# Adding the last stage's result to a tensor that already lies in the output: an accumulating DMA in place of load, add and store

## The chip, the cores and the metric

The kernel runs on one core of a Trainium2 chip. The metric is device time in microseconds, from the first to the last instruction with what lies around them; the figure for a kernel is the median over several runs. All engines of the core take part: TensorE (PE) for products, VectorE (DVE), ScalarE (ACT) and GpSimd (POOL) for elementwise work, SyncE (SP) for issuing transfers, and 16 DMA engines that carry every transfer, whichever queue issued it.

## The reference

Input x has shape (8, 256, 56, 56) in float32. Two layers are computed, each as a residual on top of a group norm `_gn`:

```
x1  = x  + involution(gn(x))             # 7x7 involution, 16 groups
out = x1 + block(gn(x1))                 # two convolutions with ternary weights

def block(v):
    out1 = relu(batch_norm(conv_tri(v, w1), g1, b1))
    out2 = batch_norm(conv_tri(out1, w2), g2, b2)
    return relu(out1 + out2)
```

`batch_norm` uses the statistics of the whole batch, so no element of `out1` is known before the first convolution has been done for all eight images, and no element of `out` before the second has. With y1 and y2 for the raw results of the two convolutions, and sc1, bi1, sc2, bi2 for the scale and bias that follow from the statistics (one pair for each channel), the last step is

```
out = x1 + relu(sc2*y2 + bi2 + relu(sc1*y1 + bi1))
```

## The kernel before

The work is done in four stages, one after the other. Stage 1 computes the involution image by image and quarter by quarter of the channels, with GpSimd, VectorE and ScalarE around the products, and stores its result x1 (`store_x1`, L888) into tensors in DRAM. Stages 2 and 3 are the two convolutions (`conv_phase`, L356), each over 16 half images. They load x1 or y1 from DRAM (`load`, L345), transform it (a Winograd form along the rows), multiply on TensorE, and store y1 or y2 to DRAM (L565). The results have to lie in DRAM because the batch's statistics come at the end of a stage[...].

The last stage, from L1079, is the one that the change touches. It runs over 16 tiles, one for each image b and half t of the channels. A tile has 128 partitions (channels) and 3136 columns (the 56 x 56 points), 1568 KB. The last two tiles are cut along the columns, into two and four pieces, so that the tail is short. For each piece it

- loads y1, y2 and x1 by three DMAs from SP's queue (L1098),
- applies scale, bias and ReLU to y1 on ScalarE (L1099),
- forms sc2*y2 + y1 on VectorE, in place in y1 (L1100),
- applies the bias and ReLU on ScalarE (L1101),
- adds it to x1 on VectorE (L1102), in place in x1,
- stores x1 to the output by a DMA from ScalarE's queue (L1103).

y1 and y2 have two buffers each and x1 three. They lie in four pools, fa to fd, placed one behind the other from the bottom of the memory that stage 3 leaves; `homes` (L1083) says which tile of which tensor lies in which pool: fd takes the first of each tensor, fa, fb and fc the others. Where a pool lies decides what it waits for at the start: the memory under it holds stage 3's loaded rows (rawp), its weights (wqa with the first four groups, wqb with the last two), the padded image (pad) and temporaries (tmpp). In the kernel before, fd lies over pad and tmpp, which are free before the last products are; fb lies over wqa.

The order of instructions on each engine is set by the Tile scheduler in this stage, engine by engine, with semaphores for data and buffers. SP's queue works in order: a load that waits for its buffer holds up those behind it.

Of the kernel before, what the change touches and what calls it, by code (L numbers as in the profile page):

```python
# [11 lines left out]
ALU = mybir.AluOpType  # L12
# [5 lines left out]
P = 128  # L18
B, C, H, W = 8, 256, 56, 56
HW = H * W  # L20
CT = C // P
# [68 lines left out]
def involution_tri_block_kernel(  # L90
# [3 lines left out]
    nc = tc.nc  # L94
    out = out.rearrange("b c h w -> b c (h w)")
# [5 lines left out]
    def scratch(name):  # L101
        return [[dram.tile([P, HW], F32, tag=f"{name}_{b}_{t}", name=f"{name}_{b}_{t}")
                 for t in range(CT)] for b in range(B)]

    x1_d, y1_d, y2_d = scratch("x1d"), scratch("y1d"), scratch("y2d")
    wq_d = [dram.tile([P, QS * CT * 3 * C], F32, tag=f"wqd{i}", name=f"wqd{i}") for i in range(2)]


# [970 lines left out]
    with ExitStack() as ph4:  # L1079

        fa, fb, fc, fd = (ph4.enter_context(tc.tile_pool(name=name, bufs=1))
                          for name in ("fa", "fb", "fc", "fd"))
        homes = {"y1": (fd, fa), "y2": (fd, fb), "x1": (fd, fb, fc)}  # L1083

        def home(name, j):
            k = j % len(homes[name])
            return homes[name][k].tile([P, HW], F32, tag=f"{name}{k}", name=f"{name}f_{j}")


        for j in range(B * CT):  # L1090
            b, t = j // CT, j % CT
            y1f, y2f, x1f = (home(name, j) for name in ("y1", "y2", "x1"))
            n = {B * CT - 2: 2, B * CT - 1: 4}.get(j, 1)
            f = HW // n
            for cols in (slice(k * f, (k + 1) * f) for k in range(n)):
                y1, y2, x1 = y1f[:, cols], y2f[:, cols], x1f[:, cols]
                for v, src in ((y1, y1_d), (y2, y2_d), (x1, x1_d)):
                    nc.sync.dma_start(v, src[b][t][:, cols])  # L1098
                nc.scalar.activation(y1, y1, AF.Relu, bias=bi1[:, t:t + 1], scale=sc1[:, t:t + 1])  # L1099
                nc.vector.scalar_tensor_tensor(y1, y2, sc2[:, t:t + 1], y1, ALU.mult, ALU.add)  # L1100
                nc.scalar.activation(y1, y1, AF.Relu, bias=bi2[:, t:t + 1])  # L1101
                nc.vector.tensor_tensor(x1, x1, y1, ALU.add)  # L1102
                nc.scalar.dma_start(out[b, t * P:(t + 1) * P, cols], x1)  # L1103


# [84 lines left out]
```

## Time and profile before

| | |
|---|---|
| median of 3 runs | 2163.53 us (2159.11 to 2166.13) |
| the profiled execution: time | 2164.76 us |
| the profiled execution: span, first to last instruction | 2163.0 us |
| DVE busy in the whole span | 1753.4 us (81%) |
| DMA traffic | 440.06 MB in 156250 packets, mean 203 GB/s |
| HBM read, written | 323.28 MB, 112.20 MB |
| last product (L522) ends, last stage's first y1f step on DVE (L1100) | 1927.3 us, 1933.03 us |
| L1099, L1100, L1101, L1102 from 1936 us on: busy | 43.5, 56.6, 47.7, 55.3 us |
| the same on a whole tile | 3.00, 3.48, 2.91, 3.43 us |
| loads of a whole tile y1f, y2f, x1f: issue to landing, median | 14.4, 18.6, 25.2 us |
| store of a whole tile out_y: issue to landing, median | 11.8 us |

The profile is one execution as the hardware profiler recorded it. "Busy" is the time in which an engine executed instructions, without the instructions that only issue transfers. A row such as `L1100 DVE ... y1f<-y2f,sc_bn,y1f` names the line of the kernel, the engine, and what is written from what. "Issue to landing" runs from the instruction that issues a transfer to the moment at which its semaphore says that all of it has arrived, with the time that it stands behind other transfers. The DMA share is the mean busy share of the 16 DMA engines in a stretch of time; GB/s counts each byte moved once.

### The profile page before, as it was taken

The numbers are of one execution on the slowest core, as the hardware profiler recorded it, in microseconds if no ns is written. First come the engines' busy times: TensorE is split into PE (matmuls) and PEld (weight loads), VectorE is DVE, ScalarE is ACT, GpSimd is POOL, SyncE is SP. The second block draws the span as 40 slices with busy tenths as digits, with TensorE's granted clock in tenths as the row PEclk, the third lists the DMA queues.
The fourth block names the chain that finished last, engine by engine and source line by source line (L and its number), as shares of the span: only waits on it lengthen the run. The fifth ranks groups of instructions, "written<-read, shape, count | busy, mean of one in ns | idle before, by whom it ended". The sixth has DMA issues, their size and how long they took to land.

```text
span 2163.0 us, 70724 instructions
## 1 busy us (share of the span) xinstructions
PE 1759.3 (81%) x29680; PEld 1632.6 (75%) x29680; DVE 1753.4 (81%) x3337; ACT 1432.2 (66%) x3553; POOL 590.7 (27%) x965
## 2 busy tenths in 40 slices
PE   4988988989899898988699999997999999960000
PEld 4777777878777687777699999997999999960000
DVE  5777978787777868877699999998999999984444
ACT  3877787877767677777366666665566666653344
POOL 0555566555546646666200000000000000000000
PEclk9999999999989999999799999998999999985555
DMA  5667777686767758667733333335323333369999
GB/s 184 212 178 232 220 211 236 195 266 197 244 185 218 239 164 263 191 203 201 254 122 122 122 122 122 122 122 189 118 114 124 124 128 128 124 262 425 429 428 397
DMA packets 156250, 440.06 MB, mean 203 GB/s; under 512 B 63774, under 2 KB 74012, under 8 KB 148508
## 3 DMA queue, kind: packets, MB, share of 16 engines
q1 hardware_dynamic: 150336, 405.50, 55.2%
q10 hardware_dynamic: 5596, 30.03, 3.3%
q8 instruction: 235, 3.85, 0.8%
q14 instruction: 83, 0.68, 0.1%
HBM read 323.28 MB, written 112.20 MB: 201 GB/s over the span
## 4 chain that ended last, share of the span: by engine, by line
PE 68%; DMA 10%; DVE 9%; issue 6%; POOL 3%; ACT 3%; ACTq 0%; SPq 0%; POOLq 0%; DVEq 0%
PE c L522 40%; PE pg L820 14%; PE pa L852 8%; PE pk L713 3%; DMA y1f<-y1d 3%; DMA x1f<-x1d 2%; PE ks L786 2%; DMA out_y<-x1f 2%; POOL q L751 1%; DVE x1f L1102 1%; DVE inv L864 1%; ACT a L824 1%; DMA y2f<-y2d 1%; POOL x L868 1%; DMA q<-in_x_nb 1%
## 5 line engine op out<-in xcount | busy, mean ns | idle before, releaser
L522 PE MATMUL c<-pl,wq 128*128 128x392 f32 x4608 | 857.7, 348 | 14.9 <-ACT pl L392 14.9
L522 PEld LDWEIGHTS c<-pl,wq 128*128 128x128 f32 x4608 | 855.7, 190 | 16.7 <-ACT pl L392 15.3
L824 ACT ACTIVATE a<-pg,bt 126x126 f32<-126x126 f32 (+1 forms) x2048 | 530.1, 469 | 110.1 <-PE pg L820 109.5
L820 PE MATMUL pg<-kr,wl 64*126 64x140 f32 (+1 forms) x6144 | 466.1, 296 | 41.2 <-issue 16.4
L820 PEld LDWEIGHTS pg<-kr,wl 64*126 64x126 f32 x6144 | 405.5, 198 | 67.2 <-issue 24.3
L852 PE MATMUL pa<-a,q 126*32 126x48 f32 x17024 | 290.4, 215 | 67.0 <-issue 52.6
L852 PEld LDWEIGHTS pa<-a,q 126*32 126x32 f32 x17024 | 242.1, 116 | 135.4 <-issue 83.6
L828 DVE TENSOR_TENSOR a<-pg,bt 126x504 f32<-126x504 f32 (+4 forms) x640 | 280.9, 480 | 54.4 <-PE pg L820 52.8
L868 POOL TENSOR_TENSOR x<-x,inv 128x168 f32<-128x168 f32 x320 | 167.0, 522 | 404.1 <-DVE inv L864 370.7
L864 DVE SCALAR_TENSOR_TENSOR inv<-pa,gn1s,inv 128x168 f32<-128x168 f32 (+1 forms) x384 | 134.2, 351 | 154.6 <-ACT inv L862 151.1
L392 ACT CAST pl<-r 128x812 fp32r<-128x812 f32 x192 | 162.5, 868 | 143.4 <-DVE r L387 122.8
L372 POOL MEMSET xp<- 128x116 f32 x32 | 6.3, 196 | 826.1 <-DVE a L387 826.1
L751 POOL TENSOR_TENSOR q<-q,sides 126x256 f32<-126x256 f32 (+1 forms) x320 | 225.5, 705 | 3.1 <-DMA q<-in_x_nb 3.1
L393 DVE TENSOR_TENSOR pl<-r,pl 128x812 fp32r<-128x812 f32 x192 | 186.6, 998 | 27.6 <-ACT pl L392 26.3
L457 ACT ACTIVATE dummy<-y,nc 128x1568 f32<-128x1568 f32 (+1 forms) x128 | 200.2, 1564 | 4.8 <-DVE y L542 3.5
L862 ACT ACTIVATE inv<-pa,gn1s 128x168 f32<-128x168 f32 x320 | 134.9, 423 | 69.5 <-PE pa L852 49.3
L149 DVE BATCH_NORM_STATS2 st<-x 128x6 f32<-128x392 f32 x256 | 137.8, 554 | 16.4 <-DMA x<-in_x 10.1
L800 POOL TENSOR_TENSOR x<-x,add 128x504 f32<-128x504 f32 (+1 forms) x128 | 127.2, 1024 | 25.4 <-ACT add L794 25.4
L1049 ACT ACTIVATE xp<-raw,gn 128x392 f32<-128x392 f32 (+1 forms) x124 | 82.5, 721 | 61.3 <-DVE a L387 61.0
L1069 ACT ACTIVATE xp<-raw,bi_bn,sc_bn 128x392 f32<-128x392 f32 (+1 forms) x124 | 82.3, 720 | 58.8 <-DVE a L387 57.1
L1100 DVE SCALAR_TENSOR_TENSOR y1f<-y2f,sc_bn,y1f 128x3136 f32<-128x3136 f32 (+2 forms) x20 | 56.6, 2831 | 64.6 <-DMA y2f<-y2d 50.6
L713 PE MATMUL pk<-x,wrn 64*128 64x168 f32 (+1 forms) x1152 | 101.0, 316 | 0.0
(174 smaller groups left out, 1789.2 us busy)
## 6 DMA issues: line engine op xcount, KB each, us to landing
q<-in_x_nb SPq DMA_DIRECT2D x320, 448.0 KB, 4.2
raw<-x1d SPq DMA_DIRECT2D x32, 812.0 KB, 5.9
raw<-y1d SPq DMA_DIRECT2D x32, 812.0 KB, 6.1
x<-in_x SPq DMA_DIRECT2D x64, 392.0 KB, 5.3
x1d<-x SPq DMA_DIRECT2D x64, 392.0 KB, 5.2
y1d<-y SPq DMA_DIRECT2D x30, 784.0 KB, 3.7
y2d<-y SPq DMA_DIRECT2D x30, 784.0 KB, 3.4
y1f<-y1d SPq DMA_DIRECT2D x14, 1568.0 KB, 14.4
```

The source lines that it names most:

```text
L392: nc.scalar.copy(hi, r)
L393: nc.vector.tensor_tensor(lo, r, hi.bitcast(F32), ALU.subtract)
L457: nc.scalar.activation(dst, v, f, bias=shift[:, to:to + 1], accum_out=stats[:, to, j, n:n + 1])
L522: nc.tensor.matmul(ps[:, to, :NM], wq[k][:, t, dx, to * P:(to + 1) * P], part[:, t, :, dx:dx + W], start=(c == 0), stop=(c == last))
L713: nc.tensor.matmul(ps[h][:, :m * W], wrn[rows, c, :], src[rows, r0:r0 + (m - 1) * PY + 1:PY, :], start=(c == 0), stop=(c == NCQ - 1))
L751: nc.gpsimd.tensor_tensor(v, v, z, ALU.add)
L820: nc.tensor.matmul(dst, wl[rows, c, gp, o:o + NQ], kr[py][rows, px, :], start=True, stop=True)
L824: nc.scalar.activation(dst[:, g + 1, p0 + j], ps[1][:NQ, j * nt + t0:j * nt + t1], AF.Identity, bias=bt[:, c, g + 1, p0 + j:p0 + j + 1])
L828: nc.vector.tensor_tensor(dst[:, g, p0:p0 + n].rearrange("q p t -> q t p"), ps[0][:NQ, t0 * n:t1 * n].rearrange("q (t p) -> q t p", p=n), ...
L852: nc.tensor.matmul(ps[o:o + m, k * w:(k + 1) * w], q[:NQ, k, o:o + m], av[:, t + k, g * w:(g + 1) * w], start=True, stop=True)
L864: nc.vector.scalar_tensor_tensor(iv, parts[:, :, g], scale[:, g:g + 1], iv, ALU.mult, ALU.add)
L868: nc.gpsimd.tensor_tensor(xv, xv, iv.rearrange("p t (y x) -> p y t x", x=PX), ALU.add)
```

## The change

x1 no longer has tensors of its own in DRAM. It is stored into the output tensor, and stages 2's loads of x1 read it from there. In the last stage x1 is not loaded and not added on VectorE: y1, which holds the rest of the sum after L1101, is sent to the output by a DMA with `accum_op=ALU.add`, issued from GpSimd's queue, which adds it to what lies there. The argument `max_dma_last_dim` limits a piece of a transfer to 1568 floats, so a row of 3136 goes as two pieces. The third buffer in fc, which was x1's, is given to y1: y1 has three buffers, y2 two, and fd holds two tiles instead of three, so fc and fd lie lower in memory than before: fc over wqa, fd over wqb and pad.

```diff
-    x1_d, y1_d, y2_d = scratch("x1d"), scratch("y1d"), scratch("y2d")
+    y1_d, y2_d = scratch("y1d"), scratch("y2d")
+    x1_d = [[out[b, t * P:(t + 1) * P, :] for t in range(CT)] for b in range(B)]
...
-        homes = {"y1": (fd, fa), "y2": (fd, fb), "x1": (fd, fb, fc)}
+        homes = {"y1": (fd, fa, fc), "y2": (fd, fb)}
...
-            y1f, y2f, x1f = (home(name, j) for name in ("y1", "y2", "x1"))
+            y1f, y2f = (home(name, j) for name in ("y1", "y2"))
...
-                y1, y2, x1 = y1f[:, cols], y2f[:, cols], x1f[:, cols]
-                for v, src in ((y1, y1_d), (y2, y2_d), (x1, x1_d)):
+                y1, y2 = y1f[:, cols], y2f[:, cols]
+                for v, src in ((y1, y1_d), (y2, y2_d)):
                     nc.sync.dma_start(v, src[b][t][:, cols])
                 nc.scalar.activation(y1, y1, AF.Relu, bias=bi1[:, t:t + 1], scale=sc1[:, t:t + 1])
                 nc.vector.scalar_tensor_tensor(y1, y2, sc2[:, t:t + 1], y1, ALU.mult, ALU.add)
                 nc.scalar.activation(y1, y1, AF.Relu, bias=bi2[:, t:t + 1])
-                nc.vector.tensor_tensor(x1, x1, y1, ALU.add)
-                nc.scalar.dma_start(out[b, t * P:(t + 1) * P, cols], x1)
+                nc.gpsimd.dma_start(out[b, t * P:(t + 1) * P, cols], y1, accum_op=ALU.add,
+                                    max_dma_last_dim=4 * min(f, HW // 2))
```

The order of the instructions on the engines, as the scheduler sets it, is the same before the last stage. In the last stage, tile 1 comes before tile 0 on VectorE and in the accumulations; SP issues y1 of tile 1, the last two y2 stores, y2 of tile 1, y1 of tile 2, then y1 and y2 of tile 0; GpSimd has nothing between its last memset of the convolution and the first accumulation. One line is added near the top, so the lines after it have numbers that are higher by one.

## The prediction, made before the changed kernel had run

> **What bounds the kernel now.** Only the last stage changes its work, so I read first the page's slices, to see when that stage runs and what is full in it:
>
> ```profile
> PE   4988988989899898988699999997999999960000
> DVE  5777978787777868877699999998999999984444
> ACT  3877787877767677777366666665566666653344
> POOL 0555566555546646666200000000000000000000
> DMA  5667777686767758667733333335323333369999
> GB/s 184 212 178 232 220 211 236 195 266 197 244 185 218 239 164 263 191 203 201 254 122 122 122 122 122 122 122 189 118 114 124 124 128 128 124 262 425 429 428 397
> ```
>
> A slice is 54 us. In the last four TensorE is silent, DVE and ACT are under half busy, GpSimd does nothing, and the DMA row stands at 9: the stage is bound by transfers. Second, the windows, for the rate in the stage's steady part, and beside it five microseconds of the convolution in which the engines are as full:
>
> ```profile
> core 0: us, PE busy (x) PEld busy (x) DVE busy (x) ACT busy (x) POOL busy (x), PEclk, DMA share, GB/s
> 1861.00:1866.00 5.00, 5.00 (x29) 5.00 (x28) 5.00 (x6) 5.00 (x7) 0.00 (x0) 1.00 1.01 360
> 1953.00:2143.00 190.00, 0.00 (x0) 0.00 (x0) 88.42 (x27) 77.01 (x28) 0.00 (x0) 0.50 1.01 427
> ```
>
> The last stage moves rows of 12,544 bytes at 427 GB/s with a DMA share of 1.01. The window at 1861 holds loads whose rows are 6,496 bytes (812 KB over 128 partitions): the same full engines move only 360 GB/s. So a full engine pays 427/360 = 1.19 times as much for a byte in half-length rows. Third, the waits from 1936 us on:
>
> ```profile
> ACT y1f L1099 <- DMA y1f<-y1d: 69.8, 16, 10.6
> ACT y1f L1101 <- DVE y1f L1100: 61.2, 18, 5.0
> DVE y1f L1100 <- DMA y2f<-y2d: 50.6, 13, 5.5
> DVE x1f L1102 <- DMA out_y<-x1f: 27.6, 7, 4.0
> ```
>
> Columns: who waited for whom, total us, times, longest. The heads of both compute engines' loops wait for loads; the rest is the chain inside a tile. Last, the timeline of SP's queue shows when the stage's loads begin:
>
> ```profile
> 1910.71 0.80 SPq L565 DMA_DIRECT2D y2d<-y  x2
> 1912.33 0.32 SPq L1098 DMA_DIRECT2D y1f<-y1d  x1
> 1912.70 1.25 SPq L1098 DMA_DIRECT2D y2f<-y2d  x1
> 1914.00 0.92 SPq L1098 DMA_DIRECT2D x1f<-x1d  x1
> 1918.43 0.32 SPq L1098 DMA_DIRECT2D y2f<-y2d  x1
> 1918.79 0.43 SPq L1098 DMA_DIRECT2D x1f<-x1d  x1
> ```
>
> **The unit.** A tile is 128 x 3136 floats, 1.606 MB; at 427 GB/s it takes 3.76 us. A tile of output costs four such units now (y1, y2, x1 in, out), 15.04 us. The timeline agrees: L1099 starts at 2010.09 and, seven tiles later, at 2115.35, which is 15.04 us each. The whole stage agrees too: from 1912.33 there are 47 loads, 16 stores and one tile of last y2 stores left, 64 units or 240.6 us, which ends at 2152.9; the span ends at 2163.0, so some 10 us are gaps at the start and the tail at the end.
>
> **What the Trainium skill says.** "DMA: Bandwidth & Descriptors", section "Issuing engines are not separate DMA queues": transfers issued from SP, ACT and GpSimd run on the same 16 engines and interleave. So moving the store to GpSimd's queue gives no bandwidth. The trace of before has no transfer from GpSimd to test it. "Collectives: The Full Stack", section "The bandwidth ceiling: the fold count and why AG ≠ RS ≠ AR": an adding transfer reads two sources for each write, both on the same read ring, and a reducing transfer measured 62.28/32.35 = 1.93 times as long as a copy. No run here shows it yet; it is the central unknown. "DMA: Bandwidth & Descriptors", "Anatomy of one DMA — SWDGE (gpsimd) path" puts about 2 us of fixed time on such a transfer; here the last out_y, 392 KB or 0.94 us of data, is issued at 2159.63 and the span ends 3.4 us later, so fixed time is about 2.4 us on ACT's queue too.
>
> **The change part by part.**
> Removed: 20 loads of x1 (16 tiles, 16 units), 20 plain stores (16 units), 20 DVE additions, 55.3 us busy. The additions are worth nothing but the last one's 0.98 us, because DVE waits for loads; in their absence DVE would wait longer for y2. The store issues on ACT (0.36 us each) likewise.
>
> Added: the accumulating transfer, 16 tiles in 20 instructions. It reads y1 from SBUF, reads out in HBM and writes out. Call its price a units a tile. From below: if the destination's read cost the engine nothing, a = 1. Two reads at the full rate: a = 2, or 1.93 by the skill. But the changed line also cuts a row into two pieces of 1568 floats, 6,272 bytes, near the rows of the 1861 window; with that window's 1.19, a = 2 x 1.19 = 2.37. From above: if read, add and write of a piece don't overlap, the source's and the destination's reads and the write stand behind each other and the add's own turn adds something, a = 3 to 4. I take 2.37, the only value that uses both a reason for two reads and this trace's own rate for pieces of this length. HBM traffic gives no relief: three tiles read and one written, before and after.
>
> Moved: stores go past nothing on GpSimd, whose last memset is at 1881.91. An accumulation waits there for the final ReLU (L1101), and behind it stand only later accumulations. Who waits for it: SP, because a y1 buffer now comes free only when the accumulation has landed, where before the DVE addition freed it. SP is in order, so a y2 load can stand behind such a wait. Is three y1 buffers enough? One turn is load about 10 us, ACT, DVE and ACT 3.0 + 3.5 + 2.9 = 9.4, some 6 of waiting between them, and an accumulation that shares the engines, about 2 x 2.37 x 3.76 = 18: 43 us. Three buffers at the transfers' pace, (2 + 2.37) x 3.76 = 16.4 us a tile, allow 49. So transfers stay the bound.
>
> Moved too: the pools. The pool fd holds two tiles, not three, and slides down onto wqb, the weights of the last two matmul groups; y1 and y2 of tile 0 can be loaded only after the last matmul, 1927.35, not at 1912.33. Instead y2 of tile 1 and y1 of tile 2 go at 1918.4. The x1 that now lies in out has the same rows of 12,544 bytes and the same stores and loads earlier in the kernel: I cost that at nothing, since those transfers have the same shapes and the convolution runs with a DMA share near 0.35.
>
> **The sum.** From 1918.4 the queues hold 31 loads (all but y1 of tile 1) and one tile of y2 stores: 32 units, 120.3 us. Accumulations: 16 x a x 3.76 = 60.2 a; at 2.37, 142.6. Gaps: 1.0 start of the first load, 1.5 until the last matmul frees wqb (two loads end at about 1926.9, the next begin at 1928.4), about 2 before the first accumulation, about 1.5 when y2 stands behind y1 on SP, and 2 of landing at the end: 8. Span: 1918.4 + 120.3 + 142.6 + 8 = 2189.3. The profiled execution took 2164.76 for a span of 2163.0, so 1.8 lie outside; its time is 1.2 above the median 2163.53. So 2189.3 + 1.8 - 1.2 = 2189.9, say 2190: 1.2% slower. In general 2047.3 + 60.2 a. Break-even is a = 1.93.
>
> **Rivals.**
> Faster: the destination's read is hidden, because source and destination are read from different memories at once, so an accumulation costs one write's worth. a = 1 to 1.19 gives 2107.5 to 2118.9; at a = 1 three buffers pace the stage at about 12 us a tile instead of 11.3, which adds some 4: 2111. It decides from a below 1.82. For it: four units became three transfers. Against it: the 1.93 of the skill. Chance 0.20.
> No change: two reads, but no loss by the shorter pieces, a = 1.9 to 2.0: 2161.7 to 2167.7. The transfers that go are paid back by the second read. For it: the skill's ratio is exactly the break-even. Against it: 360 against 427 GB/s. Chance 0.12.
> Much slower: the addition stands in the way, as read, read and write that don't overlap. a = 3 gives 2227.9, a = 4 gives 2288. For it: nothing in this trace; against it: the skill's 1.93. Chance 0.20.
> GpSimd becomes the bound: it must write descriptors for 256 pieces a tile; beyond 16.4 us a tile, 64 ns a piece, it would set the pace, and at 20 us a tile the stage would add 15 x 3.6 = 54: 2244. The trace has no such instruction. Chance 0.05.
>
> **How the numbers follow.** My case, a from 2.05 to 2.7 (2171 to 2210), has 0.43. A measurement of this kernel tells about 0.3%, 6.5 us, from no change. Faster 0.20, same 0.12, slower 0.43 + 0.20 + 0.05 = 0.68. The range takes in most of both outer cases: 2114 to 2280; my own case's is 2171 to 2210.
>
> **What would show it.** In the profile after: L1099 starts every 16.4 us; the DMA share stays at 1.0 while DVE is under a third busy; the waits name the accumulation or the loads; an accumulation takes over 12 us to land. I am wrong if tiles come every 11 to 12 us (hidden read), 15 (no price for short pieces), 19 or more (a serial addition), or if the DMA share falls well under 1 while GpSimd's queue is full.

## The result, and the profile after

| | before | after |
|---|---|---|
| median (11 runs each, side by side) | 2162.17 us | 2172.12 us |
| ratio, with its 95% interval | | 1.0052 (1.0035 to 1.007) |
| profiled execution: span | 2163.0 us | 2173.9 us |
| last product ends | 1927.31 us | 1925.55 us |
| from there to the end of the span | 235.7 us | 248.4 us |
| DMA traffic | 440.06 MB | 414.36 MB |
| HBM read, written | 323.28, 112.20 MB | 297.59, 112.20 MB |

The change makes the kernel 0.5% slower; 1.2% was forecast. The last product ends at slightly different times from execution to execution, in kernels whose earlier stages are the same. So the time from the last product's end to the end of the span, called the stage's length below, is the better measure for a single profiled execution: 12.7 us more than before. A second profile of the changed kernel, below, gives 11.0 us, so a difference of two us between single profiles tells nothing.

The slices of the page of the changed kernel (a slice is 54.3 us), a window from its middle, the engines' waits from 1936 us on, and the longest wait of SP's queue in the stage:

```profile
DVE  5777879786777869776799999998999999952122
ACT  3877787877777687776366666665666666743333
POOL 0565566555655555566100000000000000000001
DMA  5667777686757758576633333335333333379999
GB/s 183 212 188 231 209 229 235 187 259 198 259 176 244 215 171 262 175 208 200 230 121 121 121 121 121 121 140 189 121 121 121 121 121 122 120 274 295 307 325 247
```

```profile
core 0: us, PE busy (x) PEld busy (x) DVE busy (x) ACT busy (x) POOL busy (x), PEclk, DMA share, GB/s
1970.00:2140.00 170.00, 0.00 (x0) 0.00 (x0) 40.09 (x12) 66.85 (x25) 14.08 (x12) 0.50 1.02 312
```

```profile
POOL out_y L1103 <- ACT y1f L1102: 265.5, 20, 59.4
DVE y1f L1101 <- DMA y2f<-y2d: 116.0, 12, 22.7
ACT y1f L1102 <- DVE y1f L1101: 73.1, 15, 13.6
ACT y1f L1100 <- DMA y1f<-y1d: 70.6, 14, 15.3
DVE y1f L1101 <- ACT y1f L1100: 57.2, 5, 22.3
SPq L1099 <- DMA out_y<-y1f: 171.0, 13, 18.7
```

The DMA row is still 9 in the stage's slices and the share 1.02, while VectorE falls from four tenths to about two: the work that was taken away was not what the stage waited for. The window shows 312 GB/s instead of 427, with an accumulated byte counted once. If a load still takes one unit of 3.76 us, three counted tiles take the time of 3 x 427/312 = 4.11 units, so an accumulation takes 2.11. The page's row of GpSimd's queue (queue and kind: packets, MB, share of 16 engines' span) says nearly the same:

```profile
q0 software_dynamic: 4672, 25.69, 5.9%
```

5.9% of 2173.9 us is 128.3 us, 8.02 us for each of the 16 tiles, or 2.13 units of 3.76 us. SP's queue shows the start of the stage:

```profile
1908.96 0.80 SPq L566 DMA_DIRECT2D y2d<-y  x2
1916.67 0.32 SPq L1099 DMA_DIRECT2D y2f<-y2d  x1
1917.04 8.90 SPq L1099 DMA_DIRECT2D y1f<-y1d  x2
1925.99 17.36 SPq L1099 DMA_DIRECT2D y2f<-y2d  x3
```

With the last product 1.8 us earlier than in the execution of before, the first load at 1916.67 is the one that the prediction put at 1918.4, and y1 of tile 0 goes after the last product, as it said. From that load to the end of the span are 257.2 us; 32 plain units are 120.3, sixteen accumulations at 8.02 are 128.3, and 8.6 are left for gaps, where the prediction had 8. So the whole miss seemed to lie in the price of an accumulation, 2.37 forecast and 2.13 found. The experiments test what that price consists of, and why the factor 1.19 for short rows did not apply.

### The profile page after: what moved, and what is told of

The parts are those of the page before. It is cut to its first block, busy times and chain, and to the rows that moved or that the text cites. A ratio compares the mean times of both kernels' runs of the same rounds, so it can differ in the third digit from the quotient of the medians.

```text
span 2173.9 us, 70672 instructions
## 1 busy us (share of the span) xinstructions
PE 1746.6 (80%) x29680; PEld 1617.6 (74%) x29680; DVE 1700.7 (78%) x3317; ACT 1434.7 (66%) x3553; POOL 612.9 (28%) x985
## 2 busy tenths in 40 slices
DMA packets 155161, 414.36 MB, mean 191 GB/s; under 512 B 63454, under 2 KB 73692, under 8 KB 151004
## 3 DMA queue, kind: packets, MB, share of 16 engines
HBM read 297.59 MB, written 112.20 MB: 189 GB/s over the span
## 4 chain that ended last, share of the span: by engine, by line
PE 67%; issue 12%; DVE 8%; DMA 5%; POOL 4%; ACT 3%; ACTq 0%; POOLq 0%; SPq 0%; DVEq 0%
PE c L523 39%; PE pg L821 14%; PE pa L853 8%; PE pk L714 4%; DMA out_y<-y1f 2%; PE ks L787 2%; POOL q L752 1%; ACT a L825 1%; DVE inv L865 1%; DVE a L829 1%; POOL x L869 1%; DMA y1f<-y1d 1%; DVE st L150 1%; POOL out_y L1103 1%; DMA y2f<-y2d 1%
## 5 line engine op out<-in xcount | busy, mean ns | idle before, releaser
L821 PE MATMUL pg<-kr,wl 64*126 64x140 f32 (+1 forms) x6144 | 456.0, 290 | 45.4 <-issue 18.7
L821 PEld LDWEIGHTS pg<-kr,wl 64*126 64x126 f32 x6144 | 394.7, 192 | 72.7 <-issue 28.4
L393 ACT CAST pl<-r 128x812 fp32r<-128x812 f32 x192 | 162.5, 868 | 143.7 <-DVE r L388 123.1
L1101 DVE SCALAR_TENSOR_TENSOR y1f<-y2f,sc_bn,y1f 128x3136 f32<-128x3136 f32 (+2 forms) x20 | 56.5, 2831 | 177.9 <-DMA y2f<-y2d 116.0
L150 DVE BATCH_NORM_STATS2 st<-x 128x6 f32<-128x392 f32 x256 | 137.9, 554 | 15.6 <-DMA x<-in_x 9.4
## 6 DMA issues: line engine op xcount, KB each, us to landing
y1f<-y1d SPq DMA_DIRECT2D x14, 1568.0 KB, 11.4
```

The lines of the kernel that those rows point to most:

```text
L150: nc.vector.bn_stats(st[:, j, :], xt[:, j * NC:(j + 1) * NC])
L393: nc.scalar.copy(hi, r)
L821: nc.tensor.matmul(dst, wl[rows, c, gp, o:o + NQ], kr[py][rows, px, :], start=True, stop=True)
```

## The experiments

Theory A: an accumulation costs two reads, and short pieces cost next to nothing. Theory B: the second read is partly hidden, and short pieces do cost 1.19. Both give about 2.1. Theory C: the price is that of GpSimd's queue.

The last column adds up the time of all DMA packets in the trace, from SP's last two y2 stores (16.6 us before the last product ends, in every kernel) to the end of the span, for one of the 16 engines. It shows what the transfers cost the engines. Where it is less than the stage's length plus 16.6 us, the engines were idle for at least the difference. Where it is more, packets overlapped, and not all of their time reaches the end.

| kernel | ratio to before, 95% interval | stage's length, us | packets' time, us |
|---|---|---|---|
| before | | 235.7 | 249.8 |
| changed | 1.0052 (1.0035 to 1.007) | 248.4 | 259.3 |
| changed, again | 1.0065 (1.004 to 1.009) | 246.7 | 259.3 |
| plain write from GpSimd's queue | 0.9812 (0.9787 to 0.9837) | 196.5 | 199.4 |
| before, half rows | 0.9993 (0.9981 to 1.0006) | 238.2 | 254.4 |
| changed, quarter rows | 1.0053 (1.0036 to 1.0069) | 247.8 | 265.7 |
| changed, eighth rows | 1.0081 (1.0055 to 1.0107) | 254.5 | 280.6 |
| changed, pools placed as before | 1.0012 (1.0001 to 1.0023) | 239.2 | 258.3 |
| changed, four y1 buffers | 1.0033 (1.0016 to 1.005) | 245.2 | 258.8 |
| before, x1 kept in the output | 1.0001 (0.9987 to 1.0016) | 235.8 | 249.6 |
| before, tile 0 loaded from GpSimd's queue | 1.0023 (1.0008 to 1.0038) | 240.1 | 251.3 |
| changed, placed, last two tiles plain | 1.0028 (1.0013 to 1.0042) | 240.0 | 255.6 |

### Take the addition away

```diff
-                nc.gpsimd.dma_start(out[b, t * P:(t + 1) * P, cols], y1, accum_op=ALU.add,
+                nc.gpsimd.dma_start(out[b, t * P:(t + 1) * P, cols], y1,
                                     max_dma_last_dim=4 * min(f, HW // 2))
```

> The transfer from GpSimd's queue writes y1 over the output instead of adding to it, with the same pieces: the addition of x1 is left out. Theory A (an accumulation costs its two reads, short pieces cost next to nothing): the accumulation's price falls from about 2.1 units of 3.76 us a tile to about 1.05, 16 x 1.05 x 3.76 = 63 us less: about 2111 to 2117 us, a tile every 11.5 to 12 us. Theory B (the second read is partly hidden, and the short pieces cost 1.19): the write keeps 1.19 units, 54 us less: about 2119 to 2123. Theory C (what costs is GpSimd's queue and its written descriptors, not the addition): within 15 us of the changed kernel's 2172.

The ratio is 0.9812, 41 us under before and 52 us under the changed kernel (stage's lengths, 248.4 and 196.5). The row of GpSimd's queue in this kernel:

```profile
q0 software_dynamic: 4416, 25.69, 2.9%
```

2.9% of 2116.5 us is 61.4 us, 3.84 a tile: 1.02 units, for the same bytes in the same pieces from the same queue. C falls: a plain write from GpSimd's queue costs one unit. The addition is worth 8.02 - 3.84 = 4.2 us a tile, a little more than a whole unit; B's 1.19 for the plain write is not there. That this second unit is a read of the destination is not shown: the page's HBM read is 297.59 MB in both kernels, so a second read stands in no counter. What the runs show is the price.

The time falls by less than A's 63 us. The median, 2117 us, comes from a chip on which the kernel before takes 2156; set against before (0.9812 of 2163.5 us is 2123), it fits B's figure better. The packets say why. Those of GpSimd's queue take 61.4 us in the stage instead of 127.8, 66.4 less, which is A's figure. SP's transfers, nearly all of them loads, take 134.0 us instead of 127.5 for the same bytes, and the engines are idle for 13.7 us instead of 5.7; 66.4 - 6.5 - 8.0 = 51.9 is the difference of the two stages. A write is issued every 12.7 us from the third to the fourteenth whole tile, not every 11.5 to 12. That three buffers for y1 leave the engines short of work when the transfers are that cheap is likely, but was not tried separately.

### Half rows, and nothing else

```diff
-                    nc.sync.dma_start(v, src[b][t][:, cols])
+                    nc.sync.dma_start(v, src[b][t][:, cols], max_dma_last_dim=4 * min(f, HW // 2))
...
-                nc.scalar.dma_start(out[b, t * P:(t + 1) * P, cols], x1)
+                nc.scalar.dma_start(out[b, t * P:(t + 1) * P, cols], x1,
+                                    max_dma_last_dim=4 * min(f, HW // 2))
```

> The kernel before with every load and store of the last stage cut into the same pieces of 1568 floats, nothing accumulated. Theory A: half rows cost next to nothing in this stage, so within 10 us of before. Theory B: 14 whole tiles of 4 transfers pay 1.19, 56 x 0.19 x 3.76 = 40 us more: about 2202 us, and the DMA engines move about 360 GB/s in the stage's middle.

The ratio is 0.9993 (0.9981 to 1.0006): B's 40 us are excluded. The window in the stage's middle:

```profile
1953.00:2143.00 190.00, 0.00 (x0) 0.00 (x0) 88.43 (x28) 75.51 (x28) 0.00 (x0) 0.50 1.02 422
```

422 GB/s against 427 with whole rows: 1.2%, not 19%. So what were the 360 GB/s of the convolution? The trace of before answers it. These are the five microseconds that the prediction used, one by one:

```profile
1861.00:1862.00 1.00, 1.00 (x7) 1.00 (x6) 1.00 (x2) 1.00 (x2) 0.00 (x0) 1.00 1.14 332
1862.00:1863.00 1.00, 1.00 (x8) 1.00 (x7) 1.00 (x2) 1.00 (x3) 0.00 (x0) 1.00 0.89 229
1863.00:1864.00 1.00, 1.00 (x7) 1.00 (x6) 1.00 (x2) 1.00 (x3) 0.00 (x0) 1.00 0.98 383
1864.00:1865.00 1.00, 1.00 (x8) 1.00 (x7) 1.00 (x2) 1.00 (x2) 0.00 (x0) 1.00 1.03 422
1865.00:1866.00 1.00, 1.00 (x7) 1.00 (x6) 1.00 (x2) 1.00 (x2) 0.00 (x0) 1.00 1.04 435
```

SP had issued two y2 stores at 1857.46 and two loads from 1858.57 on. The low rates are at the beginning, where the stores end and the loads begin; from 1864 on, the loads run at 422 and 435 GB/s. The same can be seen with no stores just before, in windows of one microsecond after SP issued two loads at 1728.13:

```profile
1729.00:1730.00 1.00, 1.00 (x7) 1.00 (x6) 1.00 (x2) 1.00 (x1) 0.00 (x0) 1.00 0.96 130
1730.00:1731.00 1.00, 1.00 (x8) 1.00 (x7) 1.00 (x2) 0.97 (x3) 0.00 (x0) 1.00 0.88 325
1731.00:1732.00 1.00, 1.00 (x7) 1.00 (x6) 1.00 (x2) 1.00 (x3) 0.00 (x0) 1.00 0.98 409
1732.00:1733.00 1.00, 1.00 (x7) 1.00 (x6) 1.00 (x3) 1.00 (x3) 0.00 (x0) 1.00 1.05 435
```

The share is 0.96 from the first microsecond, and the rate rises from 130 to 435 GB/s over four. The single packets of the trace agree: a row of 6,496 bytes takes an engine 247 ns once the burst runs, but up to 1.28 us in the first microsecond. A busy share counts a packet from its beginning to its end, and at the head of a burst most of that time cannot be the moving of its bytes. A row of 12,544 bytes takes 469 ns in the last stage, so a byte of the shorter row costs 1.02 times as much, not 1.19. The prediction read the change from two transfers to the next two as a price for each short row.

### More pieces in an accumulation

```diff
-                                    max_dma_last_dim=4 * min(f, HW // 2))
+                                    max_dma_last_dim=4 * min(f, HW // 4))
```

and with `HW // 8`.

> The changed kernel with pieces of 784 floats in the accumulation, twice as many. Theory A with a small fixed price a piece (the 0.09 units above 2 are 21 ns for each of the 16 pieces that an engine has of a tile): 5 us more than the changed kernel, about 2177. Theory B (each halving costs 1.19): the accumulation goes from 2.1 to 2.5 units, 24 us more, about 2196.

> The changed kernel with pieces of 392 floats in the accumulation, four times as many. Theory A with 21 ns a piece: 2.36 units, 16 us more than the changed kernel, about 2188. Theory B: 2.1 x 1.19 x 1.19 = 3.0 units, 53 us more, about 2225. If GpSimd's writing of descriptors set the pace, its issue time of 1.2 us a tile would grow fourfold and the time by more than either.

The rows of GpSimd's queue, first with quarter rows, then with eighth rows:

```profile
q0 software_dynamic: 8512, 25.69, 6.1%
```

```profile
q0 software_dynamic: 16704, 25.69, 6.8%
```

6.1% of 2165.0 and 6.8% of 2166.0 us are 8.25 and 9.21 us a tile, after 8.02 with half rows: 0.24 us for 16 more pieces on each engine, then 0.95 for 32 more, some 15 and 30 ns a piece. The shares are rounded to 0.1%, which is 0.14 us a tile, so these two do not differ clearly. B wanted 2.5 and 3.0 units, 9.5 and 11.4 us. In the times, quarter rows change nothing that can be told (1.0053 beside 1.0052 and 1.0065), and eighth rows cost about 0.2 to 0.3%, 4 to 6 us, not A's 16. A's price for a piece has the right size in the packets' time, which grows by 21 us with eighth rows (280.6 against 259.3), but the stage grows by only 6 to 8. The rest is overlap: 280.6 us of packets stand in 271.1 us, so packets overlapped in an engine. GpSimd's issue of a tile takes 1.19 us with half rows, 1.28 with quarter and 1.54 with eighth rows (medians), so it never came near the pace of a tile.

### The pools placed as before, and a fourth buffer

```diff
         homes = {"y1": (fd, fa, fc), "y2": (fd, fb)}
+        fb.tile([P, HW], F32, tag="space", name="space4")
```

and, in another kernel,

```diff
-        homes = {"y1": (fd, fa, fc), "y2": (fd, fb)}
+        homes = {"y1": (fd, fa, fc, fd), "y2": (fd, fb)}
```

> The changed kernel again, beside the next three on one chip: about 0.5% over before.

> The changed kernel with one empty tile more in pool fb, so that fd lies over the padded image and the temporaries, as in the kernel before: tile 0's loads need not wait for the last product. By the sum, the loads of tile 0 move from about 1927 to about 1912 and the two gaps of the DMA engines before 1928 (about 4 us between the y2 stores and the first load, 1.5 us before wqb is free) are filled: 4 to 6 us less than the changed kernel. If the late start is hidden, nothing.

> The changed kernel with four buffers for y1 instead of three. Theory A (the DMA engines are full, the wait for a buffer is queueing): within 3 us of the changed kernel, though SP's wait of 171 us for accumulations falls. Rival (SP's wait for an accumulation to land sets the pace): 10 us or more less.

The empty tile in fb moves fc and fd up to where they were in the kernel before, and changes the order in which SP loads the first tiles. The placed version is at 1.0012 (1.0001 to 1.0023) and the changed kernel, on the same chip, at 1.0065 (1.004 to 1.009): 0.53% less, 11 us; the stage is 7.5 us shorter than in the changed kernel's second profile. That is more than the 4 to 6 expected. The windows of the changed kernel about the stage's start (the last number but one is the DMA share, and the last product ends at 1925.55):

```profile
1910.00:1915.00 5.00, 5.00 (x29) 5.00 (x28) 2.27 (x3) 4.46 (x6) 0.00 (x0) 1.00 0.75 304
1915.00:1920.00 5.00, 5.00 (x28) 5.00 (x28) 2.48 (x4) 2.40 (x3) 0.00 (x0) 1.00 0.46 140
1920.00:1925.00 5.00, 5.00 (x28) 4.98 (x28) 4.90 (x8) 4.07 (x8) 0.00 (x0) 1.00 1.00 421
1925.00:1930.00 5.00, 0.55 (x4) 0.22 (x2) 3.88 (x17) 0.33 (x4) 0.00 (x0) 0.85 0.90 286
```

and of the placed version, whose last product ends at 1921.04:

```profile
1905.00:1910.00 5.00, 5.00 (x29) 5.00 (x28) 2.76 (x3) 4.93 (x6) 0.00 (x0) 1.00 0.98 336
1910.00:1915.00 5.00, 5.00 (x29) 5.00 (x28) 1.99 (x3) 2.41 (x4) 0.00 (x0) 1.00 1.00 422
1915.00:1920.00 5.00, 5.00 (x29) 4.98 (x28) 4.90 (x8) 3.65 (x5) 0.00 (x0) 1.00 1.01 432
1920.00:1925.00 5.00, 1.04 (x6) 0.70 (x4) 4.14 (x17) 3.31 (x5) 0.00 (x0) 0.91 0.86 273
```

The hole before the last product (0.46) is closed. In the idle share it is worth 0.25 x 5 + 0.54 x 5 + 0.10 x 5 = 4.5 us in the changed kernel against about 1 in the placed one. A second hole lies later, and is closed too; first the changed kernel, then the placed one:

```profile
1980.00:2000.00 20.00, 0.00 (x0) 0.00 (x0) 10.37 (x3) 12.41 (x5) 2.39 (x2) 0.50 0.93 311
1980.00:2000.00 20.00, 0.00 (x0) 0.00 (x0) 6.65 (x2) 11.01 (x4) 2.39 (x2) 0.50 1.02 358
```

The table accounts for the whole. The packets take 259.3 us in both profiles of the changed kernel and 258.3 in the placed one, so the transfers cost nearly the same; they fill 265.0 and 263.3 us there and 255.8 here. So nearly all of the gain is engines that stand idle less and overlap more. In time, most of the 0.5% was the place of two pools. The price of the accumulations is still there: the placed version has 8.5 us more of packets' time than before, in a stage that is only 3.5 us longer.

The fourth buffer gives 1.0033 (1.0016 to 1.005), whose interval overlaps the changed kernel's, and a stage 1.5 us shorter; SP's wait for accumulations falls from 171.0 to 158.3 us. The accumulations now go at an even pace, seven of them from 1997.70 to 2091.26 us, 15.6 us apart: 4.15 units, an accumulation of 2.15. The rival's 10 us are not there in the profile; whether the buffer is worth nothing or a few microseconds the times don't tell.

### x1 in the output

The first part of the change alone (x1 stored into the output and loaded from there), in the kernel before.

> The kernel before with x1 stored into the output and loaded from there, nothing else changed. By the prediction this costs nothing: within 3 us of before.

1.0001 (0.9987 to 1.0016): where x1 lies costs nothing that can be measured, as the prediction had it.

### Two tries at a faster kernel

```diff
-                    nc.sync.dma_start(v, src[b][t][:, cols])
+                    (nc.gpsimd if j == 0 else nc.sync).dma_start(v, src[b][t][:, cols])
```

> The kernel before with tile 0's three loads issued from GpSimd's queue, which is empty, so that they don't stand behind the last but one y2 stores on SP's queue. The DMA engines are idle from about 1895 to 1911 us; the padded image and the temporaries are free at about 1907. If the stage is only bound by transfers, its loads start up to 5 us earlier and the kernel takes up to 5 us less than before (ratio about 0.998). If the y2 stores and the last product set the start anyway, no change.

It is slower, 1.0023 (1.0008 to 1.0038). GpSimd's timeline in this kernel:

```profile
1909.38 0.72 POOL L1098 DMA_DIRECT2D y1f<-y1d  x1 [30.73 <-DVE pl L393]
1910.10 0.54 POOL L1098 DMA_DIRECT2D y2f<-y2d  x1
```

The first load waits there for VectorE's last use of a temporary (L393), 14.4 us before the last product ends, where SP's was issued 15.0 us before it. So not the queue but the memory was late. The stage is 4.4 us longer, 1.5 of it in the packets' time and the rest idle; which change in the order of the loads causes this was not tried.

```diff
+                if end:
+                    x1 = fc.tile([P, f], F32, tag=f"x1_{j}_{cols.start}", name=f"x1f_{j}_{cols.start}")
+                    nc.sync.dma_start(x1, x1_d[b][t][:, cols])
...
+                if end:
+                    nc.vector.tensor_tensor(x1, x1, y1, ALU.add)
+                    nc.scalar.dma_start(out[b, t * P:(t + 1) * P, cols], x1)
+                else:
+                    nc.gpsimd.dma_start(out[b, t * P:(t + 1) * P, cols], y1, accum_op=ALU.add,
+                                        max_dma_last_dim=4 * min(f, HW // 2))
```

Here `end` holds for the last two tiles, and fd lies high because fc holds x1.

> The changed kernel with fd lying higher again, and with the last two tiles handled as before: x1 loaded, added on VectorE, stored plainly; the other 14 accumulate. If an accumulation costs 2.14 units and some 3 us more to land than a plain store, the stage from the last product's end takes about 235 to 237 us, against 239 us for the placed version and 248 for the changed kernel, and the time is within 3 us of before. If the end costs nothing extra, it stays at 239.

240.0 us, not under 239.2: the expectation fails. The last accumulation of the changed kernel is issued at 2167.11, 6.8 us before the end of the span, where the last plain store had 3.4. Here the last store has 3.4 again and the packets take 2.7 us less than in the placed version, but the stage is no shorter. The test is not a clean one: fc lies one tile lower than in the placed version and fd one tile higher, so the order of the loads differs too. No version tried beats the kernel before; the placed one is 0.12% slower (0.01 to 0.23%).

## Why the prediction was right or wrong

**What bounds the stage: right.** The share is 1.02 after, though VectorE's additions are gone. VectorE and ScalarE wait for loads, and SP waits for accumulations.

**The price of two transfers for one accumulation: right.** 8.02 us with the addition, 3.84 without, 2.09 times as much. The ratio that the prediction took from the Trainium skill ("Collectives: The Full Stack", section "The bandwidth ceiling: the fold count and why AG ≠ RS ≠ AR"), 1.93, is that of an AllGather's rate to a ReduceScatter's; it is near and slightly low for this case, and this trace's measurement decides. The page's reason, two source reads, fits the price, but no counter here shows the second read. The sentence that HBM has three tiles read before and after is not borne out by the pages either: HBM read falls by 25.7 MB, one tensor. The faster rival, in which the addition costs nothing, falls; so does the much slower one, with 3 to 4 units.

**The factor 1.19 for short pieces: wrong, and this is the step that failed.** The prediction's term was "a = 2 x 1.19 = 2.37", so "142.6" us for sixteen accumulations; measured are 2.13 and 128.3. The 1.19 came from a comparison of rates in two windows with equal DMA shares, on the belief that equal shares mean equally running engines. The windows of one microsecond show that they don't, and half rows in the kernel before cost nothing in time (0.9993) and 4.6 us in the packets' time, 1.8%. The hundredths above 2 that remain, 0.13 units or 0.49 us a tile, are about what 15 to 30 ns for each of an engine's 16 pieces give. The prediction's own sign for "no price for short pieces" was a tile every 15 us; with four y1 buffers, where the pace is even, it is 15.6.

**The sum: right with that term exchanged.** 2047.3 + 60.2 x 2.13 = 2175.5 us; the ratio 1.0052 on the 2163.53 of the time before is 2174.8. The miss of 15 us is 60.2 x 0.24 = 14.4.

**The break-even at 1.93: right, but it hides the split.** It contained the late start of tile 0. With the pools placed as before the stage is 3.5 us longer than before, with an accumulation of the same 5.9% share. Sixteen accumulations cost 16 x 0.13 x 3.76 = 8 us more than load and store, which agrees with the 8.5 us of packets' time that the placed version has more than before. The other 5 us are won back because its packets, 258.3 us, more than fill its 255.8 us, while those of the kernel before, 249.8 us, leave 2.5 of 252.3 idle.

**Three buffers: right for this price, not for the rival's.** With the plain write, which is what a hidden read would cost, tiles came every 12.7 us and the engines were idle for 8 us more, so the rival's 12 was still too fast.

**GpSimd as the bound: far off.** 1.19 us of issue for a tile, where 16.4 would have been needed.

**The chances.** Slower was right and the result lies at the lower end of the forecast case's own range (2171 to 2210), which began at a = 2.05. That is in part luck. The reason given for a price clear of break-even, the 1.19, does not hold; a price of 2.0 was listed under the rival "no change". What made the kernel slower was the late start of tile 0, which the sum had, and hundredths for each piece, which it did not single out.

## What to carry to other kernels

In a stage that is full of transfers, an addition made by the DMA is not free. Here it cost a little over one transfer more, so that replacing load, add and store by it turned the time of four transfers into that of slightly more than four, and freed only engines that were waiting. When such an edit changes the buffers, look at where the pools come to lie: here the place of two pools made most of the difference in time. Take rates from windows in which the engines are in full flow; a busy share near 1 at the head of a burst does not say that the engines run at their rate. And separate what the transfers cost from the time in which the engines stand idle: the packets' time and the stage's length need not move together.

## What the runs showed of the hardware that was not expected

- A DMA share of 0.96 stood beside 130 GB/s in the first microsecond of two loads, and 1.05 beside 435 in the fourth: a packet of 6,496 bytes took up to 1.28 us at the head of a burst and 247 ns once it ran.
- Rows cut into halves of 6,272 bytes moved at 422 GB/s, whole rows at 427.
- Accumulating a tile costs the engines 2.09 times what writing it costs, in the same pieces; for a single piece of 6,272 bytes the medians are 487 and 239 ns. GpSimd's issue takes longer too: 1.19 us against 0.72 us (medians over whole and part tiles) for the same 256 pieces.
- From the issue of the last 392 KB to the end of the span: 6.8 us with an accumulation, 4.3 with a plain write from GpSimd's queue, 3.4 with a plain store from ScalarE's queue.
- With accumulating pieces of 1,568 bytes, 280.6 us of packets' time for each engine stood in 271.1 us: packets overlapped.
